# Seven quarter products for A11 B11 in matrices 1 to 3, and a narrower count in the edge index of a relational graph layer

## The chip, the cores and the metric

The kernel runs on one core of one Trainium2 chip. The metric is device time in microseconds (us) of one execution. Five engines work side by side, each with a queue that runs in order: PE (TensorE, matrix products), DVE (VectorE), ACT (ScalarE), POOL (GpSimd) and SP (SyncE, which only issues DMAs here). ACT and POOL issue DMAs too.

## The reference

There are 1250 nodes with 1024 features, 20000 edges and 8 edge types, all in float32 and int32.

```python
h = jnp.maximum(_layernorm(x, axis=-1), 0.0)
# _rgcn(h):
msgs = x[src]
out = x @ root + bias
for r in range(weight.shape[0]):                       # 8 types
    mask = (edge_type == r).astype(x.dtype)
    sums = jax.ops.segment_sum(msgs * mask[:, None], dst, num_segments=n)
    cnt = jax.ops.segment_sum(mask, dst, num_segments=n)
    out = out + (sums / jnp.maximum(cnt, 1.0)[:, None]) @ weight[r]
# u = out
z = jnp.concatenate([u, x], axis=1) @ w_gate + b_gate
h = jnp.tanh(u) * z + x * (1.0 - z)
# returned: x + h
```

In `_rgcn` the name `x` stands for the normalized `h`. A node's mean over the edges of one type needs the number of such edges at the node.

## The kernel before

**Products.** The kernel turns the sum around: it multiplies the nodes' rows by each of the eight weights first, stores the results in DRAM (`y`), and then gathers, for every node, the product rows of its edges, scaled by one over the count of that node and type. Eleven matrices are multiplied: weights 0 to 7, then root (8), and the two halves of the gate (9 and 10). `step(s, i)` (L550) multiplies matrix `s` with block pair `i`; the 1250 rows are ten blocks of 128, in five pairs (`i` from 0 to 4).

`product` (L389) computes one such pair of blocks times a 1024x1024 matrix as a two by two product of halves, with seven products in place of eight (Winograd's form of Strassen's scheme). The left factors are `A11, A12, A22, S1` to `S4`; the right ones are the matrix's quarters and the sums `t1` to `t4`, which DVE makes. One of the seven is four matmuls of 128x512 (L405); a float32 matmul is two passes of TensorE. The names `p1` to `p7` (and the last one, on `A22`) are these seven. After each comes `done()` (L409), which calls `between(j)`; `step` uses that to place everything else in the order of the engines' queues. The order is thus written out by hand: what is issued in `between` stands in each engine's queue behind that product's own copy or addition.

**A second level.** In matrices after the first, pairs 0-1 and 2-3 go together (`paired`, L531). The product `A12 B21` of two pairs is taken by seven products of quarters, 128x256 matmuls with two of them each (class `Second`, L187; all such matmuls are recorded at L218). In matrices 4 to 9 (`thirds`, L535) `S4 B22` goes the same way (class `Third`), and so does `A11 B11` (class `First`, L320). `First` is made in three moves. `sums` and `next_sums` let DVE form sums of quarters (L272 to L281) in four small tiles, `room`. `early` (L340) runs at the end of the step before: four of the quarter products, with two copies by ACT (L344, L346) and an addition by DVE (L349). `late` (L351) runs in the first step of the two: three quarter products, with a copy by ACT (L354) that spreads one of them into both halves of a bank. Its two banks then stand where `p1`'s product would, so that `p1` only copies. `next_first` (L542) says which use comes next: pair 2-3 from step 1 of the same matrix, pair 0-1 from the last step of the matrix before.

**PSUM** has eight banks: four called `ps` (`bank()`), two `ps_b` (`lead()`), one `ps_n`, one `ps_q`.

**Edge index.** While matrices 0 to 3 are multiplied, the edges are sorted into a table of slots per node. `columns` (L932) makes columns of keys (group and node), rows and types; types 0 to 4 are group 0 and types 5 to 7 are group 1. `slots` (L997) goes through 157 chunks of 128 edges, four chunks a round, two calls of `between` a round. In each round TensorE counts edges (L1031: 20 node blocks of both groups and 80 columns of type and node block, 100 in all) and looks up (L1082) how many edges with the same key came earlier; DVE keeps running sums (L1036), splits them into two parts that bfloat16 holds exactly (L1059), multiplies and adds the looked-up parts (L1087, L1091) and compares keys within the chunk (L1096); ACT makes one-hot matrices (L1013, L1015, L1072, L1073) and casts (L1051, L1053, L1066). POOL scatters the edges' rows into the table in DRAM (L1110), one indirect DMA per chunk. The 80 columns end as counts per node and type, whose reciprocals are written into the same table rows, beside 28 slots. `order` (L1127) then ranks nodes by their number of edges (L1164), so that nodes with many edges share a block.

**Gathering.** In matrix 4 the table rows are read back (`rows_and_weights`, L748, on POOL) and `slot_weights` (L730, DVE) makes each slot's factor from the reciprocals. From matrix 5 on, POOL gathers product rows (L1294) and DVE adds them (L1299). Nodes with more than 28 edges are served by passes that run only if they are needed (L1443), behind a number that every engine loads (L1441); with these inputs they are skipped.

## Time and profile before

| what | value |
|---|---|
| runs shown | 1346.52, 1349.76 and 1345.81 us; median 1346.52 |
| the profiled execution's own time | 1347.63 us |
| its span, first to last instruction | 1345.6 us |
| mean granted TensorE clock | 0.998 |
| PE / DVE / ACT / POOL busy | 1332.0 / 995.7 / 384.0 / 579.9 us |
| 128x512 passes of L405 into `ps_b` | 1560, 595 ns each in their own columns |
| 128x256 passes of L218 (one group of them) | 288, 381 ns each |
| counts L1031, lookups L1082 | 157 and 157 |

A pass's listed duration contains its drain, during which the next pass already runs. How long a pass holds TensorE is read from the start of one to the start of the next. A row of the timeline gives the start, the time to the end of the last, the engine, line, operation, the tiles, the form and how many follow each other without a gap; idle time ahead of it and what ended it stand in brackets.

### The profile page before, as it was taken

The numbers are of one execution on the slowest core, as the hardware profiler recorded it, in microseconds if no ns is written. First come the engines' busy times: TensorE is split into PE (matmuls) and PEld (weight loads), VectorE is DVE, ScalarE is ACT, GpSimd is POOL, SyncE is SP. The second block draws the span as 40 slices with busy tenths as digits, with TensorE's granted clock in tenths as the row PEclk, the third lists the DMA queues.
The fourth block names the chain that finished last, engine by engine and source line by source line (L and its number), as shares of the span: only waits on it lengthen the run. The fifth ranks groups of instructions, "written<-read, shape, count | busy, mean of one in ns | idle before, by whom it ended". The sixth has DMA issues, their size and how long they took to land.

```text
span 1345.6 us, 13662 instructions
## 1 busy us (share of the span) xinstructions
PE 1332.0 (99%) x4098; PEld 712.2 (53%) x4098; DVE 995.7 (74%) x2049; ACT 384.0 (29%) x852; POOL 579.9 (43%) x511
## 2 busy tenths in 40 slices
PE   9999999999999999999999999999999999999997
PEld 5444455455445545655654565565556556554443
DVE  7855976876784937524887978887788799867875
ACT  3335656565641111111221211112122111221210
POOL 0001755655563346101444646336354655625631
PEclk9999999999999999999999999999999999999999
DMA  8744665844673162133739778867878967879961
GB/s 313 271 181 145 105 135 148 209 81 124 160 183 83 49 171 53 48 126 122 234 114 349 223 254 326 310 230 268 286 260 291 343 211 234 288 275 283 345 171 59
DMA packets 106910, 271.17 MB, mean 202 GB/s; under 512 B 22692, under 2 KB 24946, under 8 KB 106704
## 3 DMA queue, kind: packets, MB, share of 16 engines
q1 hardware_dynamic: 46640, 120.01, 29.2%
q0 software_dynamic: 44064, 118.28, 27.9%
q10 hardware_dynamic: 16128, 31.98, 7.2%
q8 instruction: 32, 0.52, 0.2%
q14 instruction: 46, 0.38, 0.1%
HBM read 212.71 MB, written 75.66 MB: 214 GB/s over the span
## 4 chain that ended last, share of the span: by engine, by line
PE 79%; issue 7%; DMA 7%; DVE 4%; POOL 3%; ACT 0%; POOLq 0%; DVEq 0%; ACTq 0%
PE ps_b L405 40%; PE ps L405 17%; PE ps L218 11%; DMA got<-y,idx 5%; PE ps_n L405 3%; PE ps_b L218 2%; PE ps_q L218 2%; PE ps_q L405 1%; DVE u L1299 1%; PE ps_n L218 1%; POOL got L1294 1%; DMA got<-hr_dram,node 1%; PE ps L370 1%; DMA hr_dram<-row 1%; POOL out_dram L720 1%
## 5 line engine op out<-in xcount | busy, mean ns | idle before, releaser
L405 PE MATMUL ps_b<-w,h_op 128*128 128x512 f32 x1560 | 701.9, 595 | 1.0 <-ACT row L484 0.8
L405 PEld LDWEIGHTS ps_b<-w,h_op 128*128 128x128 f32 x1560 | 291.6, 190 | 329.2 <-issue 318.7
L1294 POOL DMA_INDIRECT got<-y,idx x193 | 246.3, 1276 | 326.4 <-DVE u L1299 195.8
L1299 DVE SCALAR_TENSOR_TENSOR u<-got,w_of,u 128x1024 f32<-128x1024 f32 (+1 forms) x193 | 247.1, 1283 | 33.8 <-DMA got<-y,idx 31.1
L405 PE MATMUL ps<-w,h_op 128*128 128x512 f32 (+1 forms) x592 | 263.4, 588 | 1.0 <-ACT row L464 1.0
L1110 POOL DMA_INDIRECT table<-row_col,at_i x157 | 177.7, 1132 | 156.4 <-DVE at_i L1106 70.3
L405 PEld LDWEIGHTS ps<-w,h_op 128*128 128x128 f32 x592 | 111.3, 190 | 125.0 <-issue 120.8
L430 DVE TENSOR_TENSOR row<-row 128x512 f32<-128x512 f32 x53 | 36.7, 693 | 72.9 <-ACT row L429 72.7
L429 ACT COPY row<-ps_b 128x512 f32<-128x512 f32 x53 | 31.0, 585 | 197.4 <-PE ps_b L405 193.4
L514 ACT COPY row<-ps_b 128x512 f32<-128x512 f32 x49 | 28.6, 584 | 200.3 <-PE ps_b L405 171.5
L405 PE MATMUL ps_n<-w,h_op 128*128 128x512 f32 x176 | 80.1, 592 | 0.0
L218 PE MATMUL ps<-w,w 128*128 128x256 f32 x288 | 71.5, 381 | 0.3 <-DVE w L211 0.3
L484 ACT COPY row<-ps_b 128x512 f32<-128x512 f32 x54 | 31.6, 586 | 135.9 <-PE ps_b L405 131.1
L218 PE MATMUL ps<-w,h_op 128*128 128x256 f32 x264 | 68.3, 381 | 0.0
L218 PEld LDWEIGHTS ps<-w,w 128*128 128x128 f32 x288 | 54.2, 190 | 21.9 <-issue 14.6
L1036 DVE TENSOR_TENSOR seen<-seen,ps_n 128x100 f32<-128x100 f32 x157 | 40.3, 257 | 30.1 <-PE ps_n L1031 10.1
L218 PEld LDWEIGHTS ps<-w,h_op 128*128 128x128 f32 x264 | 49.6, 190 | 24.3 <-issue 18.7
L1096 DVE SCALAR_TENSOR_TENSOR junk<-k_bc,key_col,before 128x128 f32<-128x128 int32 x157 | 55.1, 351 | 4.2
L453 ACT COPY row<-ps_b 128x512 f32<-128x512 f32 x54 | 31.7, 587 | 90.9 <-PE ps_b L405 82.9
L405 PEld LDWEIGHTS ps_n<-w,h_op 128*128 128x128 f32 x176 | 33.4, 190 | 39.5 <-issue 38.7
L464 ACT COPY row<-ps 128x512 f32<-128x512 f32 x37 | 21.6, 585 | 105.2 <-PE ps L405 92.6
L173 DVE TENSOR_TENSOR w<-w,w 128x2048 f32<-128x2048 f32 (+1 forms) x12 | 25.4, 2115 | 35.1 <-PE ps L405 34.9
(244 smaller groups left out, 1530.6 us busy)
## 6 DMA issues: line engine op xcount, KB each, us to landing
y<-row SPq DMA_DIRECT2D x72, 512.0 KB
w<-in_L_gnn_weight_dram ACTq DMA_DIRECT2D x21, 1024.0 KB
w<-in_L_gnn_weight_dram SPq DMA_DIRECT2D x10, 1024.0 KB
k_bc<-keys_dram SPq DMA_DIRECT2D x39, 256.0 KB
l_bc<-los_dram SPq DMA_DIRECT2D x39, 256.0 KB
w<-in_L_gnn_w_gate_dram ACTq DMA_DIRECT2D x6, 1024.0 KB
h_dram<-h_op SPq DMA_DIRECT2D x9, 512.0 KB
u<-in_L_gnn_bias_dram SPq DMA_DIRECT2D x9, 512.0 KB
```

The costliest lines, as they stand in the source:

```text
L218: nc.tensor.matmul(p, a[:, k, :], b[:, k, :], start=(fresh and k == 0), stop=(k == 1), skip_group_check=True)
L405: nc.tensor.matmul(b[:, at], aop[:, i, k, :], w.of[i][:, k, at], start=(fresh and k == 0), stop=(k == KQ - 1), skip_group_check=True)
L429: nc.scalar.copy(d, b)
L430: nc.vector.tensor_add(c22, c22, d)
L453: nc.scalar.copy(c11, b)
L484: nc.scalar.copy(c12, b)
L514: nc.scalar.copy(c21, b)
L1036: nc.vector.tensor_add(seen[j][:, i, :], was, p[:, i, :])
L1096: nc.vector.scalar_tensor_tensor(junk, o["k_bc"][:, i, :], key_col[:, c:c + 1], before, op0=OP.is_equal, op1=OP.mult, accum_out=rank[:, c: ...
L1110: ins = nc.gpsimd.indirect_dma_start(out=table[:, :], out_offset=bass.IndirectOffsetOnAxis(ap=at_i[:n, i:i + 1], axis=0), in_=row_col[:n, ...
L1294: nc.gpsimd.indirect_dma_start(out=t[:n], out_offset=None, in_=y[g][:, :], in_offset=bass.IndirectOffsetOnAxis(ap=at[:n, d, k:k + 1], axis=0),
L1299: nc.vector.scalar_tensor_tensor(u[:n], t[:n], w, u[:n], op0=OP.mult, op1=OP.add)
```

## The change

`A11 B11` of pairs 0-1 and 2-3 goes by `First` in matrices 1 to 3 too. In the index, the 80 type columns are gone; chunks are counted by group and node block alone. The four counts of a round are summed in the bank by TensorE, so that one addition on DVE updates the running sums of four chunks. Lookups and counts stand one behind the other and use halves of one bank, `ps_q`. The two bfloat16 parts are now a cast on ACT and the remainder on DVE. Addresses are computed and scattered sixteen chunks at a time. The counts per type are made later, in matrix 4, from the gathered slots (a slot holds type times 1250 plus node, so that a comparison tells its type); where a node has more slots than the table holds, a new section ahead of matrix 4's last pair (run only if needed) adds the rest. The slots' weights follow behind it.

```diff
+    def firsts(s):
+        return s > 0
     def next_first(s, i):
-        if thirds(s) and i == 1:
+        if firsts(s) and i == 1:
             return s, 2
-        if thirds(s + 1) and i == NP - 1 and s + 1 < NM - 1:
+        if firsts(s + 1) and i == NP - 1 and s + 1 < NM - 1:
             return s + 1, 0
...
-        if first and inner.holds and early is None and "first" not in fill:
-            c = inner.hold()
+        if first and head and early is None and "first" not in fill:
+            c = inner.hold() if inner else bank()
             add(c, S1, True, ks=range(KQ // 2))
             b = p1()
             p5(c)
-        elif first and inner.holds:
+        elif first and head:
...
-            if i == 0 and s > 0 and j == int(thirds(s)):
+            if i == 0 and s > 0 and j == 1:
                 fac[s].make_t4()
-            if q and i % 2 == 0 and j == 3:
+            if two and i % 2 == 0 and j == 3:
                 waiting_first[s, i].fifth_to()
-                q.sums()
+                if q:
+                    q.sums()
-            if coming and i > 1 and j == 2:
+            if coming and (i > 1 or not q) and j == 2:
                 first_sums()
...
             def count(j):
...
+                m, o = len(chunks(j)), now[j]
                 for i in range(m):
-                    nc.tensor.matmul(p[:, i, :], o["is_lo"][:, i, :], o["is_at"][:, i, :],
-                                     start=True, stop=True)
+                    nc.tensor.matmul(counted[:, i:m, :], o["is_lo"][:, i, :],
+                                     o["is_at"][:, i:i + 1, :].to_broadcast([P, m - i, NHI]),
+                                     start=(i == 0), stop=(i == m - 1), skip_group_check=True)
+
+            def add_counts(j):
+                cs = chunks(j)
+                m, k = len(cs), (cs[0] - 1) % RING
+                at = slice(cs[0] % RING, cs[0] % RING + m)
+                nc.vector.tensor_add(seen[:, at, :],
+                                     seen[:, k:k + 1, :].to_broadcast([P, m, NHI]),
+                                     counted[:, :m, :])
...
             def as_bf16(j):
+                s_b = now[j]["s_b"] = ix.tile([P, CG, 2, NHI], BF16, name="s_b", bufs=3)
+                for to, k, n in parts_seen(j):
+                    if n:
+                        nc.scalar.copy(s_b[:, to:to + n, 0], seen[:, k:k + n])
+
+            def residue(j):
+                s_b = now[j]["s_b"]
+                for to, k, n in parts_seen(j):
+                    if n:
+                        nc.vector.tensor_sub(s_b[:, to:to + n, 1], seen[:, k:k + n],
+                                             s_b[:, to:to + n, 0])
...
             for j in range(ng + 3):
-                for f, of in ((as_bf16, j - 3), (one_hots, j), (load_keys, j - 1), (as_int, j - 2),
-                              (None, None), (count, j - 1), (split, j - 2), (place, j - 3),
+                for f, of in ((one_hots, j), (load_keys, j - 1), (as_bf16, j - 2),
+                              (None, None), (look, j - 3), (count, j - 1), (pick, j - 3),
+                              (add_counts, j - 1), (residue, j - 2), (place, j - 3),
                               (to_los, j - 2), (None, None)):
...
+    def slot_counts(g, at, t, cum, to):
+        n = R0[g + 1] - R0[g]
+        nc.vector.memset(cum[:, :, 0:1], float(at.shape[2]))
+        for r in range(1, n + 1):
+            nc.vector.tensor_single_scalar(t, at, float(r * N), op=OP.is_ge)
+            nc.vector.reduce_sum(cum[:, :, r:r + 1], t, axis=AX.X)
+            yield
+        nc.vector.tensor_sub(to[:, :, R0[g]:R0[g + 1]], cum[:, :, :n], cum[:, :, 1:n + 1])
...
         def beside_group():
-            for g in range(G):
-                if g:
-                    yield from rows_and_weights(g)
-                    yield
-                    yield
-                weights(g)
+            for _ in range(4):
+                yield
+            passes_over()
+            yield
+            yield from rows_and_weights(1)
+            yield
+            yield
+            for g in range(G):
+                yield from counts(g)
+
+        def weights_of_groups():
+            as_reciprocals()
+            yield
+            for g in range(G):
+                yield from weights(g)
                 yield
             yield from passes_needed()
...
+        def counts_over():
+            over = nc.values_load(n_over[0:1, 0:1], min_val=0, max_val=E // MORE,
+                                  skip_runtime_bounds_check_because="no more passes than edges")
+            with tc.If(over > 0):
...
         while s < R0[1]:
             step(s, i, on)
             s, i = next(steps)
+            if (s, i) == (R0[1] - 1, NP - 1):
+                for _ in ready:
+                    pass
+                counts_over()
+                ready = weights_of_groups()
```

In the diff `look`, `pick` and `place` are the former `place` cut in three: the lookup's matmuls; the multiplication of what was looked up; its sum, the key comparisons and, every fourth round, the addresses and scatters. `make_t3` of the coming matrix moves from one call of `between` to the next wherever `First` comes next, by a test on `coming` that was there before.

## The prediction

> **What bounds the kernel now.** I read the page first: the engines' busy shares and the slices, then the chain, then TensorE's timeline stage by stage, because a busy share of a pipelined engine does not say whether it is fed without gaps.
>
> ```profile
> span 1345.6 us, 13662 instructions
> PE 1332.0 (99%) x4098; PEld 712.2 (53%) x4098; DVE 995.7 (74%) x2049; ACT 384.0 (29%) x852; POOL 579.9 (43%) x511
> ...
> PE   9999999999999999999999999999999999999997
> PEclk9999999999999999999999999999999999999999
> ```
>
> TensorE is busy in every slice at the full granted clock; the other engines are not. A microsecond comes off the time only if TensorE streams less or waits less; work taken from DVE or ACT counts only where TensorE waits for it.
>
> TensorE's timeline in matrix 1, beside the edge index:
>
> ```profile
> 155.47 3.60 PE L405 MATMUL ps<-w,h_op 128*128 128x512 f32 x8
> 158.90 0.34 PE L1031 MATMUL ps_n<-is_at,is_lo 128*128 128x100 bf16 x4
> 159.08 0.26 PE L1082 MATMUL ps_q<-s_b,to_lo 128*128 128x40 bf16 x4
> 159.18 7.11 PE L405 MATMUL ps_b<-w,h_op 128*128 128x512 f32 x16
> ```
>
> The second column includes the drain; what counts is start to start. Eight passes of 512 columns: 158.90 - 155.47 = 3.43 us, 0.429 each (a float32 matmul is two passes). Four counts of 100 columns take 0.18 us, four lookups of 40 columns 0.10. Nothing is idle between them. The same code as this change adds runs already in the matrices from 4 on (here in matrix 8):
>
> ```profile
> 970.73 1.03 PE L218 MATMUL ps<-w,h_op 128*128 128x256 f32 x4
> 971.60 1.03 PE L218 MATMUL ps<-inner,inner 128*128 128x256 f32 x4
> 972.46 1.03 PE L218 MATMUL ps_b<-w,h_op 128*128 128x256 f32 x4
> 973.32 1.03 PE L218 MATMUL ps<-inner,inner 128*128 128x256 f32 x4
> 974.18 3.60 PE L405 MATMUL ps_b<-w,h_op 128*128 128x512 f32 x8
> ...
> 979.34 1.03 PE L218 MATMUL ps<-inner,inner 128*128 128x256 f32 x4
> 980.20 1.03 PE L218 MATMUL ps_b<-w,inner 128*128 128x256 f32 x4
> 981.08 1.13 PE L218 MATMUL ps_b<-inner,h_op 128*128 128x256 f32 x4
> 982.04 1.88 PE L405 MATMUL ps_n<-w,h_op 128*128 128x512 f32 x4
> ```
>
> These are the seven products of quarters for one use (two pairs): 974.18 - 970.73 = 3.45 and 982.04 - 979.34 = 2.70, together 6.15 us, hand-overs to ACT and DVE included.
>
> **The change part by part.**
>
> 1. A11 B11 by quarters in matrices 1 to 3. Six uses (pairs 0-1 and 2-3 of three matrices). Each removes two products, 16 passes x 0.429 = 6.86 us, and adds the 6.15 above: -0.71, times 6 = **-4.3 us**. The built order agrees in number: 48 matmuls of 512 columns fewer (1200 to 1152), 84 of 256 more (588 to 672).
>
> 2. Counts of 20 groups alone, in 39 rounds of four chunks. Four passes of 100 columns become 80, 60, 40 and 20, summed in the bank. No row has these widths; the 100-column row is 0.045 us each and the 40-column row 0.025, so four of them cost between 0.10 and 0.18. On the line between the two rows (80: 0.038, 60: 0.032, the narrow ones 0.025 at most) it is 0.12: 39 x 0.06 = **-2.4 us**, between 0 and -3.1.
>
> 3. One of the three index columns (the type and block number) is no longer transposed: its two transposes start at 46.83 and the next product at 47.26: **-0.4 us**.
>
> 4. The wait for the parts of the lookup.
>
> ```profile
> 353.22 0.34 PE L1031 MATMUL ps_n<-is_at,is_lo 128*128 128x100 bf16 x4
> 354.93 0.26 PE L1082 MATMUL ps_q<-s_b,to_lo 128*128 128x40 bf16 x4 [1.36 <-ACT s_b L1066]
> ```
>
> The counts end by 353.40 (0.18 after their start), so 1.5 us are lost here. Now the cast on ACT stands one product ahead of its lookup, behind a split on DVE. In the change cast (ACT) and remainder (DVE) are issued a round, about two products or 7 us, ahead. This wait goes: **-1.5 us**, between 0 and -1.7 with the smallest ones. What is late next is the remainder on DVE, but DVE needs only 0.9 us for it after the counts and has the round.
>
> 5. One bank for lookups and counts. DVE's first read of the lookups now waits until the four counts behind them are done as well, 0.12 us a round, and stands before the four rank comparisons (L1096) and any sum queued behind. TensorE's next lookup waits for DVE's two reads of that bank, issued 7 us before. DVE is off the path here: cost 0, at most 39 x 0.12 = 4.7 if DVE had no slack. The Trainium skill (PSUM — Partial Sum Buffer, PSUM bank collisions raise a hardware error) says that two engines on one bank and quadrant at once raise an error instead of waiting, so that a bank must be guarded whole; that is a rule against putting these two together, its price is the wait just named, and no run here shows the error.
>
> 6. A new section run only where a node has too many edges, before the last pair of matrix 4: every engine loads a number and jumps. The like section before matrix 8 (L1441) has loads of 0.49 us on TensorE and 1.30 on SyncE, at 972.3 and 978.8; in the timeline above TensorE streams through 972.46 without a gap, because its sequencer runs ahead. Cost 0; at most the longest load, +1.3. The Trainium skill (Runtime: NRT & Kernel Launch, Instruction fetch mechanics) says that a taken branch out of the fetched pages stalls until its target is fetched; it names no time, and on TensorE the row above shows none.
>
> 7. DVE and ACT. Beside the index DVE loses the type columns (L1020, 40 x 0.48 = 19.2 us), most of the running sums (L1036, 157 x 0.257 to 40 of nearly the same size: -30), the splits (L1059, 13.1) and three in four of the small ones around the table address (L1099 to L1106, 40 x 0.6 to 10: about -18), and gains remainders (about 55 x 0.2 = 11) and per use eight sums and two additions, 4.4 + 0.8, times 6 = 31. Net about -38 us. ACT loses 16.9 (L1051, L1053), gains 6 x 1.3 of copies. Scatters to the table go out sixteen at a time, the same 157 on GpSimd; nothing else is in that queue then. In matrix 4 DVE counts types over the slots, 8 compares and 8 sums of 280 columns. The like weights (L738, L742) take 0.45 us each: 16 x 0.45 = 7.2. They stand behind group 1's gathers on GpSimd, which end at 541 in this trace; DVE comes to them at the end of the third pair of matrix 4, whose first product TensorE starts at 559.97. That cover is 19 us or more.
>
> ```profile
> 150.00:200.00 50.00, 50.00 (x182) 25.51 (x181) 39.47 (x179) 31.74 (x84) 29.51 (x29) 1.00 0.71 122
> ...
> 550.00:600.00 50.00, 50.00 (x159) 29.77 (x158) 22.84 (x68) 9.87 (x20) 0.00 (x0) 1.00 0.24 86
> ```
>
> In these rows by window (window, length, then busy us of PE, PEld, DVE, ACT, POOL) DVE has 10 us free in 50 beside the index and 27 in matrix 4. TensorE sees none of this work as long as in each use (a) ACT's copy of the first quarter product is done while the next one streams, 0.86 us, and (b) DVE's second set of sums is done before the fifth product, which stands behind a whole product and half of another: 3.43 + 1.72 = 5.1 us. For (b) DVE has 0.42 + 0.42 + 0.68 = 1.5 us to do. Its queue may hold a heavy half round of the index before that (in matrix 3, two comparisons of L1164 of 1.55), 2.6 to 3.1 us, but that begins while the first four quarter products stream (3.45). Slack about 2.4 us at the worst place. For (a) ACT's half round, up to 1.85 + 1.3 + 0.3 us (L1013 to L1073), stands before the copy; the product before gives 3.43 us to run it. Cost of both 0; without cover see the rivals.
>
> Sum: -4.3 - 2.4 - 0.4 - 1.5 = **-8.6 us**. The profiled execution took 1347.63 (span 1345.6 and 2.0 around it): 1339.0. It lies 1.1 above the median of the three runs, 1346.52, from which the same sum gives 1337.9. I say **1338.5 us**.
>
> **Rivals.**
>
> *Given back in part.* The six uses stand where both other engines are fuller than in the matrices from which I took the price (ACT 31.7 of 50 us, against 9.9 in matrix 4). If DVE's or ACT's queue is 1 us late per use, 6 us return: 1344, within 0.3%. For it: one such wait, 1.5 us, is in the trace. Against it: the queues get shorter. Points: 2.4 us of DVE lateness in matrix 3.
>
> *Slower.* ACT takes the place of the wait removed. Its copy of the first quarter product is an in-order instruction behind the index's half round, 1.85 + 1.3 + 0.3 = 3.4 us. If that half starts only when the product before ends (it waits for DVE's running sums, say), the copy ends 3.4 + 0.36 + 0.25 (the lag of ACT L344 behind the product's end, 971.85 against 971.60) after that product, while TensorE needs it 1.7 us after (two quarter products): 2.3 us lost. The same before the copy of the sixth step (L354), nearly as much: 6 x 4.4 = 26 us, so 1338.5 + 26 = 1365. It decides as soon as both are late by 1 us each (12 us): then 1350.5 is passed. Against it: ACT waits for TensorE before nearly every product copy in the index stage, so it runs ahead.
>
> *More is gained.* The counts at the 40-column price and the last small waits: another 1 to 2 us, 1336 to 1337. It lies in the forecast's range.
>
> That the change does not do what it says is ruled out by the built order's numbers in point 1.
>
> **How the numbers follow.** 0.3% of 1346.5, about what a measurement of this kernel tells from no change, is 4 us: faster is below 1342.5, slower above 1350.5. Forecast with its open terms (counts 0 to -3.1, the wait 0 to -1.7, the jump up to +1.3, and the 1.1 between the two bases): 1335.5 to 1342.5, 0.75. Given back in part: 1342.5 to 1350.5, 0.17. Slower: 0.08. The range for 8 in 10 reaches from 1335.5 into the second case, to 1345.5.
>
> **What would show it.** Point 1: groups of 128x256 on the quarter line 168 passes larger, and in matrices 1 to 3 the pieces 3.45 and 2.70 us long. Point 2: four counts in about 0.12 us. Point 4: no idle time of TensorE ended by the parts of the lookup. Point 6: no gap at the new load. Points 5 and 7: DVE busy near 965 us, ACT near 375. I am wrong if TensorE's first-quarter copies show idle time ended by ACT or DVE in matrices 1 to 3, or if gaps appear in matrices 4 and 5.

## The result, and the profile after

The changed kernel took **1353.48 us** (median of seven runs, 1349.82 to 1358.68); the kernel before took 1345.81 (seven runs, 1344.20 to 1349.76). The ratio is 1.0055 [1.0041, 1.0069] (in brackets, here and below, its 95% interval): slower by about half a per cent, where 1338.5 was forecast, and above the forecast's range. The profiled execution of after took 1350.36, one of the shorter ones. The experiments below ran in several groups, each with runs of before beside them; after itself was not run again, so a difference from 1353.48 is one between groups. In three of the groups semaphores (the counters by which one engine tells another that its work is done) came late; those groups are named where they occur, and no cause is taken from their times.

The head of the page of after, engine by engine (busy time, share, instructions), with TensorE's slices:

```profile
span 1348.5 us, 13403 instructions
PE 1325.2 (98%) x4168; PEld 721.6 (54%) x4168; DVE 957.9 (71%) x1823; ACT 378.9 (28%) x804; POOL 568.6 (42%) x509
...
PE   9999999999999999999999999999999999999997
PEclk9999999999999999999999999999999999999999
```

Every engine has less to do than before: TensorE 6.8 us less, DVE 37.8, ACT 5.1, POOL 11.3. The slices look the same. And yet the span is 2.9 us longer. So the removed work is really gone, and idle time has come that tenths of a slice of 34 us do not show. With each shape of pass taken at its median distance start to start (0.429 us for 512 columns, 0.216 for 256), TensorE's passes add up to 1318.9 us before and 1311.0 after: -7.9, a little more than the 7.1 of the prediction's points 1 to 3. What lies between them, waits and hand-overs, grew by about 10.8, where point 4 had it fall by 1.5.

The chains behind those 10.8 us begin in the list of TensorE's waits in after (who waited and for whom; us in total, times, the longest):

```profile
PE ps_q L1100 <- ACT to_lo L1093: 4.8, 4, 2.3
PE ps L217 <- DVE inner L278: 2.9, 1, 2.9
...
PE ps L217 <- DVE row L245: 1.8, 1, 1.8
```

None of these three stands in the list of before. They are two different places.

**Place one: the lookup waits for a load that ACT waits for.** In matrix 2, on TensorE, on ACT, and the load on SP's queue, each from the timeline of its engine (start, duration, engine, line; in brackets the engine's idle time and what ended it):

```profile
355.03 3.60 PE L404 MATMUL ps<-w,h_op 128*128 128x512 f32 x8
360.89 0.27 PE L1100 MATMUL ps_q<-s_b,to_lo 128*128 128x40 bf16 x4 [2.27 <-ACT to_lo L1093]
```

```profile
359.46 0.72 ACT L1092 ACTIVATE to_lo<-l_bc,less_pid 128x512 bf16<-128x512 int32 x1 [6.04 <-DMA l_bc<-los_dram]
360.21 0.63 ACT L1093 ACTIVATE to_lo<-to_lo 128x512 bf16<-128x512 bf16 x1
```

```profile
345.99 0.32 SPq L1064 DMA_DIRECT2D k_bc<-keys_dram  x1
346.36 1.30 SPq L1064 DMA_DIRECT2D l_bc<-los_dram  x1
```

Eight passes of 512 columns take 3.43 us, so the lookup could have started at 358.46; it started 2.43 later. Behind it is not ACT's work but ACT's wait of 6.04 us for `l_bc` (256 KB, a row broadcast over 128 partitions), which had been issued at 346.36: 13.1 us from issue to use. `k_bc` and `l_bc` have three buffers each, and SP issues a round's `k_bc`, then its `l_bc`, as soon as DVE has done the rank comparisons of the round that held the oldest buffer. In this trace DVE's fourth comparison of that round starts at 345.60 and its accumulator is read at 345.88; SP issues `k_bc` at 345.99. So how far ahead a load is depends on how long the rounds are. In before, 4.7 us is the shortest distance between lookups of successive rounds from matrix 2 on. In after there are distances of 2.1 us (216.11 to 218.23) and 3.7 (341.98 to 345.72). ACT waited for `l_bc` 1.4 us in before, once, and in after 25.2 us, nine times. The 1.4 is a low value: in two other traces of the same index (`held_5` and `held_14` below, which differ from before only in matrix 6) ACT waits for `l_bc` 9.7 and 10.2 us, six times each and at most 3.9, and TensorE does not stand for it. So late loads were there before; in after the waits are longer and reach TensorE. Five gaps of TensorE before lookups add up to 5.7 us (start to start; the list above counts idle time alone).

**Place two: the end of the index.** On POOL and DVE, then on TensorE:

```profile
432.00 0.90 POOL L1139 DMA_INDIRECT table<-row_col,at_i  x1 [0.30 <-issue]
432.91 0.16 POOL L1161 IOTA ids<- 128x10 int32 x1
```

```profile
433.11 0.17 DVE L1163 CAST ids_f<-ids 128x10 f32<-128x10 int32 x1 [16.79 <-POOL ids L1161]
...
442.78 1.55 DVE L1184 SCALAR_TENSOR_TENSOR junk<-v_bc,val,one 128x1280 bf16<-128x1280 f32 x1 [4.20 <-DMA v_bc<-val_dram]
```

```profile
433.79 1.03 PE L217 MATMUL ps<-w,h_op 128*128 128x256 f32 x4
436.63 1.13 PE L217 MATMUL ps<-inner,inner 128*128 128x256 f32 x4 [1.82 <-DVE row L245]
...
442.76 1.88 PE L404 MATMUL ps<-w,h_op 128*128 128x512 f32 x4
447.59 1.13 PE L217 MATMUL ps<-inner,inner 128*128 128x256 f32 x4 [2.95 <-DVE inner L278]
```

The last batch of scatters stands in POOL's queue, each 0.98 us and 0.30 to the next, 1.28 apart; the small IOTA for `ids` stands behind them. DVE stands 16.8 us before its cast of that IOTA's result, in order, and the sums of a `First` use are behind the cast. TensorE loses 1.98 us before the second quarter product and 3.11 before the fifth: start to start, 2.84 instead of 0.86 and 4.83 instead of 1.72. Part of the second loss is DVE's wait of 4.2 us for `v_bc`. That is no separate origin: `v_bc` is loaded from `val`, which DVE computes from the cast (L1167), so it is late for the same reason, and where the IOTA comes early (`ids_first`) DVE does not wait for it.

### The profile page after: what moved, and what is told of

The parts are those of the page before. It is cut to its first block, busy times and chain, and to the rows that moved or that the text cites. A ratio compares the mean times of both kernels' runs of the same rounds, so it can differ in the third digit from the quotient of the medians.

```text
span 1348.5 us, 13403 instructions
## 1 busy us (share of the span) xinstructions
PE 1325.2 (98%) x4168; PEld 721.6 (54%) x4168; DVE 957.9 (71%) x1823; ACT 378.9 (28%) x804; POOL 568.6 (42%) x509
## 4 chain that ended last, share of the span: by engine, by line
PE 78%; DMA 9%; issue 6%; DVE 4%; POOL 2%; ACT 1%; POOLq 0%; ACTq 0%; DVEq 0%; SPq 0%
PE ps_b L404 37%; PE ps L404 16%; PE ps L217 13%; DMA got<-y,idx 5%; PE ps_b L217 3%; PE ps_n L404 3%; DMA l_bc<-los_dram 2%; PE ps_q L217 2%; PE ps_n L217 1%; PE ps_q L404 1%; DMA out_dram<-row,node 1%; PE ps L369 1%; DVE u L1325 1%; POOL out_dram L726 1%; DMA hr_dram<-row 1%
## 5 line engine op out<-in xcount | busy, mean ns | idle before, releaser
L404 PE MATMUL ps_b<-w,h_op 128*128 128x512 f32 x1464 | 659.2, 595 | 1.3 <-ACT row L483 0.8
L404 PEld LDWEIGHTS ps_b<-w,h_op 128*128 128x128 f32 x1464 | 273.9, 190 | 307.9 <-issue 296.2
L1139 POOL DMA_INDIRECT table<-row_col,at_i x157 | 166.9, 1063 | 180.9 <-DVE at_i L1135 127.4
L404 PEld LDWEIGHTS ps<-w,h_op 128*128 128x128 f32 x592 | 111.1, 190 | 120.1 <-issue 116.2
L217 PE MATMUL ps<-w,h_op 128*128 128x256 f32 x288 | 74.7, 382 | 0.0
L217 PE MATMUL ps<-inner,inner 128*128 128x256 f32 x264 | 68.0, 380 | 4.8 <-DVE inner L278 2.9
L217 PEld LDWEIGHTS ps<-w,h_op 128*128 128x128 f32 x288 | 53.9, 190 | 26.0 <-issue 19.9
L217 PEld LDWEIGHTS ps<-inner,inner 128*128 128x128 f32 x264 | 50.0, 190 | 20.0 <-issue 7.4
L404 PEld LDWEIGHTS ps_n<-w,h_op 128*128 128x128 f32 x176 | 33.4, 190 | 39.5 <-issue 38.7
L1032 ACT ACTIVATE is_lo<-io,less_lo 128x128 bf16<-128x128 f32 x157 | 50.1, 391 | 3.0 <-PE ps L404 2.3
```

Of the source, the lines that this page charges most:

```text
L217: nc.tensor.matmul(p, a[:, k, :], b[:, k, :], start=(fresh and k == 0), stop=(k == 1), skip_group_check=True)
L404: nc.tensor.matmul(b[:, at], aop[:, i, k, :], w.of[i][:, k, at], start=(fresh and k == 0), stop=(k == KQ - 1), skip_group_check=True)
L1032: nc.scalar.activation(is_lo[:, i, :], io, AF.Abs, bias=less_lo[:, c0 + i:c0 + i + 1])
L1139: ins = nc.gpsimd.indirect_dma_start(out=table[:, :], out_offset=bass.IndirectOffsetOnAxis(ap=at_i[:n, c:c + 1], axis=0), in_=row_col[:n, ...
```

## Experiments

### Each part by itself

**Only the index** (`index_alone`): after, with `A11 B11` of matrices 1 to 3 left as before.

```diff
     def firsts(s):
-        return s > 0
+        return s > EARLY
...
-            if two and i % 2 == 0 and j == 3:
+            if two and i % 2 == 0 and j == 3 and firsts(s):
```

> The changed kernel with the seven products of A11 B11 held back to the matrices from 4 on, as before; the new index stays. In the changed kernel's trace TensorE loses 5.7 us to lookups that wait for ACT's one-hots of the low key parts, which wait for the load l_bc, and 5.1 us at the end of the index (434 to 448), where DVE stood 16.8 us behind GpSimd's iota and then waited for v_bc. Theory 'bunched rounds': the First uses of matrices 1 to 3 shorten some index rounds, so the loads come late only with them; then this kernel keeps the index's saving (-2.4 counts, -0.4 transposes, -1.5 old wait = -4.3) and at most the 5.1 at the end: 1345.8 - 4.3 + 0 to 5.1 = 1341.5 to 1346.6. Rival 'new index': the bursts of sixteen scatters and the later pick delay the loads whatever TensorE's pieces are; then 1345.8 - 4.3 + 5.7 + 5.1 = 1352, up to 1355.

Measured: 1341.54 against 1345.36, ratio 0.9965 [0.9951, 0.9979]; the same kernel again (`index_alone_b`) 1344.44 against 1346.16, 0.9981 [0.9965, 0.9997].

> The kernel of index_alone again (1341.5 in its first run), as the control beside the next one: if it is slow here too, the long waits belong to the chip of the call, and this and ids_keys must be judged from a call without them; if it is near 1341.5 while the next one is slow, they belong to the kernel.

The index part alone is a gain of 3.8 and 1.7 us, at most the size of points 2, 3 and 4 together (-4.3). In its first profile no wait of TensorE is left in the index stage, in the second one of 0.4 us. ACT's waits for `l_bc` are 6.6 and 9.2 us, five times each, much as in `held_5`. That the new index is what costs, the rival, fell.

**Only `First`** (`first_alone`): before, with the hunks of the diff for `First` alone (`firsts`, `head`, `next_first`, the calls in `between`, and the small tiles `room` made at the start).

```diff
+    def firsts(s):
+        return s > 0
...
-        if thirds(s) and i == 1:
+        if firsts(s) and i == 1:
...
-                b = first.late() if inner.holds else first.to1
+                b = first.late() if head else first.to1
```

> The kernel before with nothing but the seven products of A11 B11 in matrices 1 to 3 as well; the old index. If my price of a use holds under the index too (-0.71 each, six uses): 1345.8 - 4.3 = 1341.5, with idle time of TensorE as before. Theory 'bunched rounds': the same late loads show here, ACT to_lo waiting for l_bc in several rounds and TensorE losing 3 to 6 us: 1344.5 to 1347.5. Rival 'new index': no such waits here, 1341.5.

Measured: 1349.98 against the same runs of before, 1.0028 [1.0018, 1.0039]. Its own passes would make it 4.3 us faster, so waits cost some 9 us. Here ACT waits for `l_bc` twelve times, 23.7 us. In the index stage TensorE stands eight times, 7.0 us in all (once, 1.4, in before). Seven of these waits, 3.1 us, are for DVE's running sums, for the parts of the lookup, and for DVE to read the lookups' bank, so fuller engines seem to have a share here too. The largest wait stops TensorE in another way, at the place that the prediction's slower rival names. ACT and TensorE in `first_alone`, and two windows of its span (length, busy us of PE, PEld, DVE, ACT, POOL, granted clock, DMA share, GB/s):

```profile
390.72 0.72 ACT L1081 ACTIVATE to_lo<-l_bc,less_pid 128x512 bf16<-128x512 int32 x1 [5.16 <-DMA l_bc<-los_dram]
...
392.01 0.37 ACT L344 COPY ps_b<-ps 128x256 f32<-128x256 f32 x1
```

```profile
392.43 2.07 PE L218 MATMUL ps_b<-w,h_op 128*128 128x256 f32 x4 [3.87 <-ACT ps_b L344]
394.29 1.91 PE L218 MATMUL ps<-inner,inner 128*128 128x256 f32 x4
```

```profile
394.00:396.00 2.00, 2.00 (x6) 1.53 (x5) 0.79 (x3) 0.00 (x0) 1.19 (x2) 0.50 0.59 77
...
398.00:400.00 2.00, 2.00 (x6) 0.81 (x5) 2.00 (x3) 0.00 (x0) 1.70 (x2) 1.00 0.92 248
```

ACT's copy of the first quarter product (L344) is done at 392.38, behind a half round of the index that was held by its load, and TensorE stands 3.87 us. Then four passes of 256 columns take 1.86 us instead of 0.86: the granted clock is 0.50 from 394 to 396 and full again from 398 on. This wait cost more than its length.

### Each wait by itself

**The IOTA ahead of the scatters** (`ids_first`): `ids` does not depend on the table; it is filled at the start of the index.

```diff
+            nc.gpsimd.iota(ids, pattern=[[P, ND]], base=0, channel_multiplier=1)
             nc.gpsimd.iota(pid, pattern=[[0, 1]], base=0, channel_multiplier=1,
...
-                nc.gpsimd.iota(ids, pattern=[[P, ND]], base=0, channel_multiplier=1)
                 ids_f = sp.tile([P, ND], F32, name="ids_f")
```

> The changed kernel with one instruction moved: GpSimd's iota of the node numbers goes ahead of all scatters, so that DVE's cast of it at the end of the index waits for nothing. Theory 'behind the burst': the 16.8 us of DVE go and with them both TensorE gaps at the end of the index (1.98 at 434.44, 3.11 at 444.05): 1353.5 - 5.1 = 1348.4. Rival: the second gap belongs to the load of v_bc alone (4.2 us of DVE's wait) and comes back wherever that load falls: only -2.0, 1351.5.

Measured: 1342.71 (1339.81 to 1349.44), 0.9978 [0.9966, 0.9989]. Both gaps at the end of the index are gone (the second and fifth quarter products follow at 0.86 and 1.72), so the cause is the IOTA behind the scatters and not `v_bc` alone. The effect looks twice as large as expected: 10.8 us below the 1353.48 of after, where the two gaps make 5.1. That compares two groups of runs; it is 7.65 below the profiled execution of after, in which the gaps were read.

**Scatters round by round** (`scatter_by_round`): `AT = 1` instead of 4, so that four scatters go out after each round and none is held back for the last batch.

> The changed kernel with the scatters sent out every round of four chunks instead of sixteen chunks at a time (AT = 1); nothing else. Theory 'behind the burst': DVE's wait for the iota falls from 16.8 us to the 5 of the kernel before and both TensorE gaps at the end of the index go, as in ids_first: 1342 to 1344. Rival: the iota behind four scatters is still late enough, or DVE's small operations, three per round instead of per four rounds (30 rounds x 0.65 = 20 us), make the index late elsewhere: 1350 and more.

Measured: 1349.93 (1345.59 to 1363.17), 1.0011 [0.9989, 1.0032], on a chip with late semaphores. DVE's wait before the cast is 4.9 us and no gap is at the end of the index, which agrees with `ids_first`; the time by itself is not to be read there.

**Neither part alone makes place two.** In `index_alone` DVE waits 16.8 us for the IOTA too, and TensorE does not stand: whole products follow there (8, 16, 8 and 8 passes from 427.37 to 444.54), none of which needs a sum that is behind the cast. In `first_alone` the sums are there, but the cast's wait is 5.7 us, and nothing stands. Only both together put the sums of a `First` use behind a cast that comes 16.8 us late.

**Four key buffers** (`keys_four`): the loads may go a round further ahead.

```diff
-                    t = now[j][name] = ix.tile([P, CG, P], I32, name=name, bufs=3)
+                    t = now[j][name] = ix.tile([P, CG, P], I32, name=name, bufs=4)
```

> The changed kernel with four buffers instead of three for the two key loads k_bc and l_bc, so that a load is released by the rank comparisons one round earlier. Theory 'issued too late': the loads then have about 7 us more before their use (they took up to 14.5 us from issue to use where ACT waited), the waits of to_lo go: 1353.5 - 5.7 = 1347.8 in the middle, and the runs spread less than 1349.8 to 1358.7. Rival 'the DMA engines are full': an earlier load lands no earlier, 1353 as before.

Measured: 1345.50 (1343.3 to 1354.2), 1.0007 [0.9992, 1.0023]: 8.0 us below the median of after, 4.9 below its profiled execution. TensorE's waits for the lookup's key half fell from 4.8 us to 0.8, ACT's wait for the load from 25.2 (nine times) to 10.3 (twice). What is left are 0.9 us for a first-quarter copy, and the end of the index, where both gaps remained (1.97 and 3.24). So the theory holds for the lookups, and less for ACT, whose two waits are still 6.4 us at the longest; the runs spread as far as those of after, against what was expected.

**Both edits** (`ids_keys`, `ids_keys_b`, `ids_keys_c`): `ids_first` and `keys_four` in one.

> The changed kernel with both edits: the iota ahead of the scatters and four buffers for the key loads. Theory so far: the loss consists of TensorE waits of two origins, each longer when it passes about 3 us, because TensorE then runs at half the clock for some 4 us more; without both the stream is 1298.5 (its passes at their own start-to-start) + 26.1 (hand-overs and start as in index_alone) + 9.6 + 1.8 outside = 1336, at most 1340 with one small wait left, and the runs lie within 3 us of each other. Rival: the uneven rounds of the First uses cost TensorE in other places too, as the copies on ACT behind the index; then 1342 or more.

> The kernel of ids_keys once more, on another chip if it comes to that: in its first run (1390.6) ACT and DVE stood 3 to 14 us for TensorE's semaphore, which came that late after the matmul had ended, in many places that have no such wait in ids_first or keys_four. If that belongs to the chip of that call, this is 1336 to 1340, the sum of both edits; if it belongs to the kernel (both edits together bring it about), 1380 to 1396 again.

> Both edits again, beside the control. Theory: the sum of both edits, 1336 to 1340, wherever index_alone is at 1341.5. Rival: 1380 to 1400 beside an undisturbed control: then the fourth buffers together with the early iota make a new wait of their own.

Measured: 1.0284 [1.0251, 1.0317] and 1.0345 [1.0311, 1.0378] (1390.63 and 1396.54), and the third time 1343.38, 0.9969 [0.9952, 0.9987]. Two of these three groups lie on chips with late semaphores (below), and the third does not. There the version is faster than before by 0.3% and 10 us below after. `ids_first` was ahead of before by as much (0.9978), so what the four buffers add to it is within the noise. Beside `index_alone_b` in the same group (1344.44) it is 1.1 us faster, which is within the noise, where `First` saves 4.3 us in passes: most of that is still lost. It is not the 1336 that the sum of both gains would give: its `l_bc` waits are still 15.0 us in ACT, four times; one of them stands in front of a first-quarter copy (2.1 us of TensorE). Two more waits, 2.0 and 3.5 us start to start, lie far behind the index, at 991 and 1072 us, where the traces of the kernels differ in place and size of the waits.

**`First` with four `k_bc` buffers** (`first_keys`, `_b`, `_c`): `first_alone` with `bufs=4 if name == "k_bc" else 3`.

> The kernel before with the seven products of A11 B11 in matrices 1 to 3 (as first_alone) and four buffers for k_bc, whose release lets the next pair of key loads go; l_bc keeps three. Theory 'late loads': what First alone lost (1349.98 against 1341 by its matmuls) is ACT standing in front of its product copies because a key load has not landed; with the loads a round earlier it gives back most: 1341 to 1344. Rival 'heavier engines': DVE and ACT are too full beside the old index for eight sums a use; then it stays near 1350.

> The kernel of first_keys once more, for the same reason. Theory 'late loads': 1341 to 1344, with no product copy of ACT that waits behind to_lo. Rival 'heavier engines': about 1350 as in first_alone.

> first_keys a third time, for a chip without the long semaphore waits (its own matmuls give 1341). Theory 'late loads': with four buffers for k_bc it takes 1341 to 1345, against 1350 of first_alone. Rival 'heavier engines': about 1350, with TensorE waiting for DVE's sums or ACT's copies although no load is late. If the kernel before is near 1349 again and semaphores come late, the run says nothing.

Measured: 1.0074 [1.0047, 1.0101], 1.0051 [1.0035, 1.0068] and 1.0063 [1.0038, 1.0087], all three on chips with late semaphores. In the traces ACT waits for `l_bc` once or twice (3.3 to 8.3 us in all) instead of twelve times, while `scatter_by_round`, with three buffers on the same chip, still has eight such waits (22.1 us). So the fourth buffer removes most of them; the time does not tell what that is worth. Open.

### The disputed zeros

**Counts in a bank of their own** (`index_two_banks`): `index_alone` with the counts in `ps_n`.

```diff
-            counted = q_bank[:, H:H + CG * NHI].rearrange("p (c b) -> p c b", b=NHI)
+            n_bank = psum.tile([P, CG, P], F32, name="ps_n", bufs=1).rearrange("p c k -> p (c k)")
+            counted = n_bank[:, H:H + CG * NHI].rearrange("p (c b) -> p c b", b=NHI)
```

> index_alone with the counts in a bank of their own (the one they had before), so that DVE's first read of the lookups no longer waits for the four counts behind them. My price for one bank was 0, at most 39 x 0.12 = 4.7: 1341.5 means that it costs nothing, 1337 that DVE is on the path.

Measured: 1343.95, 0.9981 [0.9968, 0.9994], against 0.9965 and 0.9981 of `index_alone`. The groups lie on different chips and each interval is some 2 us wide on either side: no cost of one bank shows, and one of 1 or 2 us would not have been seen.

**No section for overflow** (`index_no_jump`, `_b`, `_c`): `index_alone` without the call of `counts_over` (the counts of edges beyond a node's slots are left out).

> index_alone without the section that is run only where a node has too many edges: the load of a number on every engine and the jump before the last pair of matrix 4 are left out, and with them what the section would compute; with these inputs it is never entered. My price 0 to +1.3: 1341.5 or down to 1340.2. Rival: it stalls the engines' fetching there and costs 2 us or more.

> The kernel of index_no_jump once more, for the same reason: the section that counts over-full nodes, its loads and its jump left out. Price of the jump 0 to +1.3, so 1341.5 down to 1340.2; if leaving it out makes the kernel slow by itself, 1366 to 1373 again.

> index_no_jump a third time, for the same reason; what it leaves out is the section for over-full nodes with its loads and its jump. 1341.5 (1344.4 on the chip of the last call) down to 1.3 less. On a chip with late semaphores again 1366 or more, and the price stays open.

Measured: 1.0140 [1.0112, 1.0169], 1.0192 [1.0169, 1.0214] and 1.0178 [1.0150, 1.0206] (1369.71 to 1375.88), all on chips with late semaphores. The time is lost in the index, far ahead of the section's place: in the first profile DVE waits 38.7 us, up to 14.0 at once and all before 371 us, for lookups and counts that TensorE had ended. `index_alone` itself was not run on these chips. From the list of DVE's waits of `index_no_jump`, and the longest of them in the timelines of DVE and POOL:

```profile
DVE own L1108 <- remote: 38.7, 5, 14.0
```

```profile
239.80 0.33 DVE L1108 TENSOR_TENSOR own<-ps_q,is_at 128x160 f32<-128x160 f32 x1 [14.00 <-remote]
```

```profile
237.25 0.98 POOL L1139 DMA_INDIRECT table<-row_col,at_i  x1 [0.30 <-issue]
```

"remote" means that no instruction of the trace ended just before the semaphore came. TensorE's lookup, which DVE multiplies here, had started at 227.54 and taken 0.26. The scatter at 237.25 is the last of a batch of sixteen. So the price of the jump was not measured by a time. In the trace of after, TensorE's load for it is at 599.8 (0.49 us long), and the quarter products there start at 598.93, 599.79, 600.66 and 601.52, without a gap.

### What a wait costs

**A held transpose** (`held_5`, `held_14`): before, with one transpose on TensorE that needs a chain of 5 or 14 copies on ACT, in matrix 6, ahead of a product of eight passes.

```diff
         two = paired(s, i)
+        if (s, i) == (6, 2):
+            for _ in range(14):
+                nc.scalar.copy(held_up, held_up)
+            nc.tensor.transpose(bank()[:, :P], held_up, ident)
...
+    held_up = const.tile([P, P], F32, name="held_up")
+    nc.gpsimd.memset(held_up, 0.0)
```

> The kernel before with TensorE held up once, in a stretch without gaps: before the third pair of matrix 6 ACT copies a small tile five times onto itself and TensorE transposes that tile. The copies begin when the last product copy is through, so TensorE waits about 0.85 + 5 x 0.25 = 2.1 us. Theory 'clock': below some 3 us nothing but the wait is lost, and the granted clock stays at 1.00 behind it. Rival: every wait of 2 us or more is followed by slow passes.

> The same with fourteen copies: TensorE waits about 0.85 + 14 x 0.25 = 4.4 us. Theory 'clock': the passes behind the wait run at half the granted clock for 3 to 4 us, 0.43 us for 256 columns instead of 0.216, so that the wait costs 6 to 8 us in all. Rival: the slow passes seen in three traces have another cause (DMA traffic, the power of all engines), and none are here: 4.4 us.

Measured, one execution each beside a before of 1347.01: 1348.15 with five copies (a gap of 2.35 us), 1354.22 with fourteen (5.3). TensorE's timeline and a window after the wait in `held_14`:

```profile
795.73 0.48 PE L556 MATMUL ps<-ident,held_up 128*128 128x128 f32 x1 [5.16 <-ACT held_up L555]
796.00 6.28 PE L405 MATMUL ps_n<-w,h_op 128*128 128x512 f32 x8
```

```profile
798.00:801.00 3.00, 3.00 (x4) 1.06 (x4) 1.28 (x1) 0.00 (x0) 2.50 (x4) 0.50 0.94 348
```

The eight passes behind it take 802.12 - 796.00 = 6.12 us instead of 3.43, at a granted clock of 0.50 up to about 801. So in the trace this wait costs its 5.3 us and 2.7 more, about 8; the one execution is 7.2 us longer than the median of before. In `held_5` the clock stays at 1.00, and the wait costs its length.

## Why the prediction was wrong

**What held.** Point 1: in matrix 2 a use takes 3.45 and 2.66 us (forecast 3.45 and 2.70). Point 2: the four counts take 0.11 (forecast 0.12). Both in TensorE's timeline of after:

```profile
260.59 1.03 PE L217 MATMUL ps<-w,h_op 128*128 128x256 f32 x4
...
264.04 3.60 PE L404 MATMUL ps_b<-w,h_op 128*128 128x512 f32 x8
267.47 0.26 PE L1100 MATMUL ps_q<-s_b,to_lo 128*128 128x40 bf16 x4
267.58 0.26 PE L1046 MATMUL ps_q<-is_at,is_lo 128*128 128x80 bf16 x4
267.69 1.96 PE L404 MATMUL ps<-w,h_op 128*128 128x512 f32 x4
269.49 1.03 PE L217 MATMUL ps<-inner,inner 128*128 128x256 f32 x4
...
272.15 1.88 PE L404 MATMUL ps<-w,h_op 128*128 128x512 f32 x4
```

264.04 - 260.59 = 3.45 for four quarter products and 272.15 - 269.49 = 2.66 for three; 0.11 from lookups to counts and 0.11 from counts to the next product. Point 4: no wait for the parts of the lookup is left (the new ones are for its keys). Point 5: no cost of one bank shows, by `index_two_banks`. Point 6: no gap at the load; by the trace alone. Point 7's amounts: DVE 957.9 (forecast 965), ACT 378.9 (375); its cover in matrix 4 held too, with no gap there. The stream at its median distances fell by 7.9 where these points had 7.1.

**What failed is point 7, twice, and with it the end of point 4.** Both times a cover was claimed for work in order on another engine.

*"Scatters to the table go out sixteen at a time, the same 157 on GpSimd; nothing else is in that queue then."* The IOTA for `ids` is in it. In before it stood behind the one scatter of the last chunk and ended at 419.98; DVE's cast came at 423.55. DVE stood 5.2 us ahead of that cast as well, but a copy of ACT is listed as what ended it, not the IOTA. Now the last batch has thirteen scatters (157 are nine times sixteen and thirteen), and DVE waits 16.8 us. The rows were at hand: scatters in before are 1.28 us apart too, and 13 x 1.28 = 16.6. To count the scatters is not enough; what has to be asked is who stands behind the last. Point 7 also gave the second set of sums a "slack about 2.4 us at the worst place", in matrix 3; it is there that DVE came 3.1 us late, since neither the cast nor `v_bc` was in that sum. Cost in the profiled execution: 5.1 us of TensorE.

*"For (a) ACT's half round, up to 1.85 + 1.3 + 0.3 us, stands before the copy; the product before gives 3.43 us to run it."* The half round was priced as work, at 3.4 us. It has a load in it, and it was never asked whether the load is there. `First` adds four quarter products (3.45 us) to the end of one step and takes two products (6.86 us) out of the next two, which get 2.66 back, so the rounds of the index, which follow TensorE's steps, become uneven: two lookups 2.1 to 3.7 us apart, then a long distance. The loads, issued only when the oldest buffer comes free, are late for the short rounds. ACT's first-quarter copy itself held TensorE in `first_alone` (3.87 us, and more by the clock), `keys_four` (0.9) and `ids_keys_c` (2.1). In the trace of after the same lateness struck the lookups, 5.7 us. So point 4 failed there too: it said that "what is late next is the remainder on DVE", and what was late next was ACT's half of the lookup's keys. `index_alone`, whose rounds are spaced as in before, waits for no lookup in one trace and 0.4 us in the other.

*"Against it: the queues get shorter."* This was the argument against "given back in part", and it misses the kind of wait. The queues did get shorter (DVE is busy 32.7 us of the 50 from 150 to 200, 39.5 before) and TensorE waited all the same, since what it waited for was not work in a queue but a load and an IOTA behind an engine's in-order wait.

**The rival "slower"** had the right place for `first_alone`, ACT's first-quarter copy behind the index's half round (the 3.87 us), though not for after, with another cause (it had DVE's running sums hold the half round) and a chance of 0.08. That after came out above its bound of 1350.5 is luck in so far as the waits were others.

**No term stood for the clock.** In the profiled execution of after the gaps of the two places make 10.8 us, and the granted clock stayed at 1.00 behind them. The other runs of after are up to 8 us longer than the profiled one. The mean granted clock that each run lists falls with the time: 0.998 at 1349.82 and 1350.36, 0.997 at 1350.52 and 1353.48, 0.996 at 1355.60, 1356.04 and 1358.68. Half clock after a wait, in some executions and not in others, is the part of it that such a mean can show; 0.002 of 1350 us is 2.7 us lost, so more than half of the spread seems to have another cause. Late semaphores in some executions are a rival that nothing here tests: only one execution of after has a trace, and it shows none. The 10.8 us that `ids_first` brought are not explained in full either: 5.1 are gaps, and the medians' clocks, 0.997 and 0.998, stand for 1.4.

What stays open: the time for the jump, what four `k_bc` buffers alone are worth, the spread of after's runs, and why waits far behind the index (1.9 us ahead of 1000.97 in after, 0.3 ahead of the same pass in before) come and go.

## What to carry to other kernels

When work is made shorter on TensorE, the side pipeline that is clocked by its steps changes its rhythm: look for the shortest round that results, and compare it with the lead of that pipeline's loads, which its buffers set. When instructions are gathered into a batch, write down what stands behind the last of them on its queue and who waits for that. A wait of 2 to 5 us on a TensorE that is otherwise never idle is to be priced at its length and, as these traces have it, up to 3 us more. And a version is to be timed on more than one chip, beside the kernel that it is compared with.

## What the runs showed of the hardware

**Half clock after a wait, but not after each.** The granted clock was 0.50 for 3.4 us, starting 0.3 to 1.3 us after the end of gaps of 2.07, 2.98, 3.19 and 3.24 us (in `index_alone_b`, `ids_first` twice, `keys_four`). In `index_alone_b` three groups of four 256-column passes then took 1.59, 1.71 and 1.08 us instead of 0.86 each: 1.8 us lost beside the gap. With gaps of 4.03 and 5.3 us (`first_alone`, `held_14`) it fell within the gap and was full again 5.5 and 5.7 us behind it, at a loss of 2.7 to 2.8 us beside the gap. It stayed at 1.00 behind gaps of 2.35, 2.43, 3.11 and 3.50 us (`held_5`, after twice, `ids_keys_c`). So the length alone does not decide. The Trainium skill (TensorE: Matmul & The Clock Gate, What's actually happening) says that the clock is halved after at least one idle window of about 3.4 us, and that the window is free-running: it does not reset when a kernel starts. A free window fits that gaps of like length end differently; that a gap of 2.07 us was enough does not fit an idle window of 3.4, and the measurement decides.

**Loads that are long on the way.** In after `l_bc`, 256 KB, took 13.1 us from issue to use where ACT stood for it, and its issue alone up to 4.1 us on SP (median 0.40), beside the other loads of the index stage.

**Semaphores that come late.** In three groups of runs, on two chips (`ids_keys`, `scatter_by_round`, `first_keys`, `index_no_jump`, and the repeats `_b` and `first_keys_c`, `index_no_jump_c`), DVE and ACT waited up to 14 us for TensorE's work that the trace shows as long ended. The kernel before lost little there (1348.89 to 1349.69 against 1345 to 1347 elsewhere), versions of the change up to 48 us. The same kernel, `ids_keys`, was 3.4% slower than before in one such group and 0.3% faster in an undisturbed one, so a single group would have told a false story.

The rows point at the scatters. All fourteen such waits of `index_no_jump` begin while POOL sends a run of scatters, and seven of them, the longest among them, end 1.6 to 2.4 us after the run's last scatter (239.80 after 238.23 above). The trace of before that the prediction reads has two of them, 4.6 us of DVE at 175.76, just as a run of eight scatters ends, and 0.9 of ACT at 299.06, 1.2 us after another. On these chips the kernels that send sixteen scatters at a time lost 20 to 48 us (`index_no_jump`, `ids_keys`); the one that sends four, `scatter_by_round`, lost 0.5, and `first_keys`, with the scatters of before, 7 to 11 (`first_alone` lost 4.6 elsewhere). But after and `index_alone` send sixteen elsewhere without one such wait, and no run changes the batch alone on such a chip. So that the change's own batches are what these chips make slow is likely and not shown, and how a scatter would delay a semaphore is not known.
